# Row tiles on TensorE: scores as two 64x128 tiles, transposes of gathered rows in halves

## The chip, the cores and the metric

The kernel runs on one core of one Trainium2 chip. The metric is the device time of one execution in microseconds; lower is better. TensorE multiplies a stationary operand (loaded first, by a weight load) with a moving operand that is streamed through it. Its 128x128 array can be used as several smaller tiles: a tile is written rows x columns, where the rows are the partitions that are summed over and the columns are the width of the stationary operand.

## The reference

One layer of graph attention over a sparse graph of 2048 nodes, for a batch of 8 and 4 heads of 64 channels, and a second attention layer with one head, then residual and layer norms. Cut to what matters here:

```python
h = jnp.einsum('bnc,hdc->bhnd', x, Wh)                  # 8 x 4 x 2048 x 64
scores = jnp.einsum('...nd,...md->...nm', h, h)
attn = softmax(where(mask, scores, -1e16), axis=-1)     # mask: adjacency and the diagonal
out_h = jnp.einsum('...nm,...md->...nd', attn, h) + bh
z = leaky_relu(heads side by side); h2 = z @ Wo.T
# the same attention once more on h2, then layer norm, residual, layer norm
```

Everything is float32. The adjacency is dense only for nodes of low number; the first 56 nodes are the "hub".

## The kernel before

The kernel never forms the projected features for the scores. With G_h = Wh_h^T Wh_h, the score of nodes n and m in head h is x_n^T G_h x_m, so the raw rows of x are the keys, and `columns` (L802 to L806) makes the queries G_h x of a node's own column. The 8 batches are held as 4 (`Q`) pairs of two (`p`), 64 channels each, so that 128 partitions hold both batches of a pair.

It runs in three parts. First (up to about 144 us in the profile) the adjacency is read and turned into lists of up to 128 neighbours for 166 sets of 12 nodes, while `hub_scores` (L585) and `hub_values` (L601) work off the hub's attention over all 16 blocks of 128 nodes. Then comes the loop at L1017 over 83 pairs of sets (`g`), the first layer. Then a third loop (L1351) does the second layer in the same manner.

The loop at L1017 is written out by hand as a software pipeline, under a manual schedule: the order of the calls is the order of each engine's queue. For pair `g`, spread over several turns:
- `gather` (L790) fetches, by an indirect DMA on GpSimd's queue, the rows of the neighbours of each of the two sets (`j`) into `rows[1, s]`, 128 rows by 4 pairs of batches.
- `turn` (L509) transposes a gathered tile with four TensorE transposes of 128x128 into a PSUM tile `tp` of two banks, one bank for each set. It is called twice in a turn, at L1078 and L1083, with `turn_values` (L863) of an older pair between. ScalarE copies `tp` into `xTg` (L1030) in the next turn.
- `scores` (L814) multiplies `xTg` (stationary) with the queries `y` (moving, 48 columns: 12 nodes x 4 heads). The 64 channels of batch `p` are partitions `half(p)`, and the output goes to bank `p`. Each product of 128 neighbours is made as two products of 64 (`r`), which go to the lower and the upper 64 partitions of the output. VectorE adds the mask (`weigh`, L826), ScalarE takes the exponential (`lift`, L833).
- `values` (L846) multiplies the weights with the gathered rows in 128x64 tiles, `invert` divides, `turn_values` (L863) transposes, `project` (L531) applies the heads' weights in 64x64 tiles, `second_maps` (L880) the second layer's weights in 128x64 tiles, `second_rows` (L890) transposes them for the second layer's table.

TensorE's order within a turn is L821 (scores of pair i+1), L531, L846, L880, L890, L806, L512 (four transposes), L863, L512 (four more). PSUM has one buffer for each of the tags T (transposes), S (scores), O and C in this loop.

`hub_scores` has the same form of product: stationary `xT` in 64 channels x 64 nodes, moving `yh` with 224 columns.

Of the kernel before, what the change touches and what calls it, by code (L numbers as in the profile page):

```python
# [30 lines left out]
F32 = mybir.dt.float32  # L31
# [328 lines left out]
def fast_kernel(ctx: ExitStack, tc: tile.TileContext, x, adj, Wh, bh, Wo, bo, gamma, beta, out, flag):  # L360


    nc = tc.nc
    B, N, C = x.shape
    H, D, _ = Wh.shape
    P = 128
    NB = N // P
    Q = B // 2
# [7 lines left out]
    M = SET * H  # L376
# [14 lines left out]
    work = stage.enter_context(tc.tile_pool(name="work", bufs=2))  # L391
# [3 lines left out]
    def two(name, tag="s", **kw):  # L395

        return psum.tile([P, 2, 512], F32, tag=tag, name=name, **kw)

    def half(k):
        return slice(k * 64, (k + 1) * 64)  # L400
# [10 lines left out]
    ident = const.tile([P, P], F32, name="ident")  # L411
# [19 lines left out]
    xT = early.tile([P, Q, N], F32, name="xT")  # L431
# [74 lines left out]
        nc.vector.tensor_copy(woT.rearrange("p q d -> p (q d)"), po[:, 0, :HP * D])  # L506


    def turn(tp, rows):  # L509

        for q in range(Q):
            nc.tensor.transpose(tp[:, q * P:(q + 1) * P], rows[:, q, 1:1 + P], ident)  # L512

    def leaky(cat, n, name):

        z = work.tile([P, HP, 2, n], F32, tag="z", name=name, bufs=3)
        for hp in range(HP):
            nc.scalar.activation(z[:, hp], cat[:, :, hp * n:(hp + 1) * n], AF.Identity, bias=bhp[:, hp:hp + 1], scale=1.0)  # L518
        return z

    def leak(z):
        f = z.rearrange("p q s n -> p (q s n)")
        nc.vector.scalar_tensor_tensor(f, f, SLOPE, f, OP.mult, OP.max)

    def project(ot, cat, n):

        for hp in range(HP):
            for s in range(2):
                for j in range(2):
                    h = 2 * hp + j  # L530
                    nc.tensor.matmul(cat[half(j), s, hp * n:(hp + 1) * n], whT[half(s), h * D:(h + 1) * D],  # L531
                                     ot[half(s), h, :], start=True, stop=True)
# [3 lines left out]
    HW = HUB * H  # L536
# [32 lines left out]
    yh = early.tile([P, 2, 2 * HUB * H], F32, name="yh")  # L569
# [15 lines left out]
    def hub_scores(i, t):  # L585
        sp = two(f"sh{i}_{t}")
        for k in range(2):
            for p in range(2):
                for r in range(2):
                    nc.tensor.matmul(sp[half(r), p, k * HW:(k + 1) * HW],  # L590
                                     xT[half(p), 2 * t + k, i * P + r * 64:i * P + (r + 1) * 64],
                                     yh[half(p), t, k * HW:(k + 1) * HW], start=True, stop=True)
        e = es[t][:, :4 * HW]
        nc.vector.tensor_tensor(e.rearrange("p (a k n) -> p a k n", a=2, k=2),  # L594
                                sp[:, :, :2 * HW].rearrange("p a (k n) -> p a k n", k=2),
                                maskh[:, i, :].unsqueeze(1).unsqueeze(1).to_broadcast([P, 2, 2, HW]), OP.subtract)
        nc.scalar.activation(e, e, AF.Exp, bias=shifts[:, 0:1], scale=1.0)  # L597
# [189 lines left out]
    rows = {}  # L787
    held = {}
# [23 lines left out]
        nc.scalar.copy(held["y", g // 2][:, :n, g % 2 * 2:g % 2 * 2 + 2], cat[:, :, 2 * GM:2 * GM + n].rearrange("p a n -> p n a"))  # L812

    def scores(g, sp):  # L814
        xt = held.pop(("T", 1, g)).rearrange("c j (q n) -> c j q n", q=Q)
        y = held["y", g // 2][:, g % 2 * GM:(g % 2 + 1) * GM, :].rearrange("p n h -> p (n h)")
        for j in range(2):
            for q in range(Q):
                for p in range(2):
                    for r in range(2):  # L820
                        nc.tensor.matmul(sp[half(r), p, (q * 2 + j) * M:(q * 2 + j + 1) * M], xt[half(p), j, q, half(r)],  # L821
                                         y[half(p), (j * Q + q) * M:(j * Q + q + 1) * M], start=True, stop=True)

    def weigh(g, sp):
        e = es[g % 2]
        nc.vector.tensor_tensor(e[:, :16 * M].rearrange("p (a q n) -> p a q n", a=2, q=Q),  # L826
                                sp[:, :, :8 * M].rearrange("p a (q n) -> p a q n", q=Q),
                                mask[:, 2 * g:2 * g + 2, :].rearrange("p s n -> p (s n)").unsqueeze(1).unsqueeze(1)
                                .to_broadcast([P, 2, Q, 2 * M]), OP.subtract)

    def lift(g):
        e = es[g % 2]
        nc.scalar.activation(e[:, :16 * M], e[:, :16 * M], AF.Exp, bias=shifts[:, 0:1], scale=1.0)  # L833
# [3 lines left out]
    def values(g, op):  # L837
        e = es[g % 2]
        rw = [rows.pop((1, 2 * g + j)) for j in range(2)]
        for q in range(Q):  # L840
            for j in range(2):
                for p in range(2):
                    c0 = (p * 8 + q * 2 + j) * M
                    o0 = q // 2 * OQ + q % 2 * (D + 2) + p

                    nc.tensor.matmul(op[half(p), j, o0:o0 + K1], e[:, c0:c0 + 64], rw[j][:, q, sums(p)], start=True, stop=True)  # L846

    def invert(g, op):
        v = op.rearrange("a j (k c) -> a (j k) c", k=2)[:, :, :2 * (D + 2)].rearrange("a w (s c) -> a w s c", s=2)
        osb = held["o", g] = work.tile([P, 4, 2, D], F32, tag="osb", name=f"osb{g}")  # L850
        r = rall[:, g, :].rearrange("a (w s) -> a w s", w=4)
        for p in range(2):
            nc.vector.reciprocal(r[half(p)], v[half(p), :, :, p * K1])  # L853
        nc.vector.tensor_tensor(osb, v[:, :, :, 1:K1], r.unsqueeze(3).to_broadcast([P, 4, 2, D]), OP.mult)  # L854
# [152 lines left out]
    def one(name, tag):  # L1007
        return psum1.tile([P, 2, 512], F32, tag=tag, name=name)
# [8 lines left out]
    for i in range(-4, NG + 3):  # L1017
        if 0 <= i + 1 < NG:
            sp = one(f"s{i + 1}", "S")
            scores(i + 1, sp)  # L1020
            weigh(i + 1, sp)
        if i >= 1 and slow and len(slow) % 3:
            slow.pop(0)()
        cat = one(f"cat{i}", "C")
        if 0 <= i - 1 < NG:
            project(held.pop(("ot", i - 1)), cat, GM)
            held["z", i - 1] = leaky(cat, GM, f"z{i - 1}")
        if 0 <= i + 2 < NG:
            t = held["T", 1, i + 2] = work.tile([P, 2, 512], F32, tag="xTg", name=f"xTg{i + 2}", bufs=3)
            nc.scalar.copy(t, held.pop(("tp", i + 2)))  # L1030
        if 0 <= i + 1 < NG:
            lift(i + 1)
        if 0 <= i < NG:
            op = one(f"o{i}", "O")
            values(i, op)
            invert(i, op)
        if 0 <= i + LOOK < NG and i > -3:
            for j in range(2):
                gather(table1, 2 * (i + LOOK) + j, 1, rows_tile)
        if i + 6 < NG and i % 2 == 0 and i >= -2:  # L1040
            own_rows((i + 6) // 2)
        if 0 <= (i - 30) // 2 <= NV:
            (add_beta if i % 2 else load_own)((i - 30) // 2)
        if 0 <= i - 1 < NG:
            leak(held["z", i - 1])
        if i >= 0:
            if turns():
                some(1)
            if slow and len(slow) % 3 == 0:
                slow.pop(0)()  # L1050
            more(1)
            if todo3 and i == todo3[0][0]:
                make_keys(2, todo3.pop(0)[1], late_two)
            if not picks:
                ready = done
            if not picks and not todo3 and done < NS:
                picks = pick(2)
                done = NS
            assert i + 1 + LOOK >= NG or 2 * (i + 1 + LOOK) + 1 < ready

        if 0 <= i - 2 < NG:
            second_maps(i - 2, cat[:, 0, 384:384 + GM])
        if 0 <= i - 3 < NG:
            second_rows(i - 3, cat[:GM, 1, 384:512])
        if 0 <= i + 4 < NG + NG % 2:
            columns(i + 4, cat)
        if 0 <= i - 2 < NG:
            keep_own(i - 2, cat[:, 0, 384:384 + GM])
        if 0 <= i - 3 < NG:
            keep_rows(i - 3, cat[:GM, 1, 384:512])  # L1070
        for _ in range((2 if i < 22 or i % 2 else 1) if i >= 0 else 0):
            if not turns():
                some(1)
        if 0 <= i + 4 < NG + NG % 2:
            keep_columns(i + 4, cat)
        if 0 <= i + 3 < NG:
            tp = held["tp", i + 3] = one(f"t{i + 3}", "T")
            turn(tp[:, 0, :], rows[1, 2 * (i + 3)])  # L1078
        if 0 <= i < NG:
            turn_values(i, op)  # L1080
            keep_values(i, op)
        if 0 <= i + 3 < NG:
            turn(tp[:, 1, :], rows[1, 2 * (i + 3) + 1])  # L1083
    assert not picks and not pieces and not todo3 and done == NS
    begin.close()
    stage.close()
# [347 lines left out]
```

## Time and profile before

| | us |
|---|---|
| median of 3 runs | 879.14 (877.95 to 882.98) |
| the profiled execution, its own time | 880.76 |
| its span from first to last instruction | 878.9 |
| PE busy in the span | 753.0 |
| PE busy between 190 and 582 us | 385.8 of 392 |
| mean granted clock of TensorE | 0.951 |

PE stands for TensorE's matmuls and transposes, PEld for its weight loads, DVE for VectorE, ACT for ScalarE, POOL for GpSimd. A row such as "PE s L821 x64" in the chain of waits means 64 instructions of line 821 that write the tile `s`. In rows of instructions "64*64 64x48" is the shape of the stationary operand and of the moving one. Matmuls overlap: a single one's duration is longer than the time between two starts, so the length of a group on the chain, or the distance between starts, tells what it costs.

### The profile page before, as it was taken

Reading aid. Unit: us, or ns where it says so; the run is one execution under the profiler, and the core shown is the slowest. Engines: PE = TensorE matmul, PEld = TensorE weight load, DVE = VectorE, ACT = ScalarE, POOL = GpSimd, SP = SyncE. Lnnn points to the kernel's source line nnn. Section 1 sums busy time; section 2 is a strip of 40 time slices with the busy share of each in tenths; the row PEclk is TensorE's granted clock in tenths of the full one; section 3 lists DMA queues with packets and bytes.
Section 4 is the critical chain, followed back from the end, with each engine's and each line's share of the span. In section 5 each row is a group of like instructions: output and inputs, shape, how many; then the busy total and the mean of one; then the engine's idle time right before and its main releaser. Section 6 shows DMA issues by size and latency. Waiting matters only on the chain.

```text
span 878.9 us, 42066 instructions
## 1 busy us (share of the span) xinstructions
PE 753.0 (86%) x18437; PEld 661.2 (75%) x18437; DVE 610.1 (69%) x1369; ACT 514.4 (59%) x961; POOL 469.2 (53%) x612
## 2 busy tenths in 40 slices
PE   1896777889999999999999999992999999998730
PEld 1664456778788999988999999971899999988720
DVE  3356983568888788877555555553258999998994
ACT  2342333556556667666766667651678888886821
POOL 5654141457444555655666666503777777777300
PEclk9998998999999999999999999995999999999965
DMA  8787451355434445655566665514888888888611
GB/s 167 238 218 213 129 146 48 83 142 160 109 100 118 112 125 159 162 169 153 160 168 173 160 166 162 134 28 114 246 266 253 275 275 267 266 252 242 172 46 35
DMA packets 81794, 145.22 MB, mean 165 GB/s; under 512 B 30146, under 2 KB 46466, under 8 KB 81602
## 3 DMA queue, kind: packets, MB, share of 16 engines
q0 software_dynamic: 26720, 88.55, 36.4%
q1 hardware_dynamic: 37842, 49.65, 18.7%
q10 hardware_dynamic: 17040, 4.25, 2.6%
q8 instruction: 147, 2.41, 1.1%
q14 instruction: 45, 0.37, 0.1%
HBM read 123.91 MB, written 18.48 MB: 162 GB/s over the span
## 4 chain that ended last, share of the span: by engine, by line
PE 63%; DVE 15%; DMA 7%; ACT 5%; issue 4%; SPq 3%; POOL 2%; DVEq 0%; ACTq 0%; POOLq 0%
PE t L512 11%; PE s L821 10%; PE o L846 10%; PE cat L806 6%; PE o L863 4%; PE cat L531 4%; PE cat L880 3%; PE s L1133 3%; PE o L1165 3%; PE cat L890 2%; DMA raw<-in_adj_dram 2%; SPq L1248 2%; PE sh L1277 2%; PE e L1144 2%; DMA g<-table,index 1%
## 5 line engine op out<-in xcount | busy, mean ns | idle before, releaser
L792 POOL DMA_INDIRECT g<-table,index x332 | 334.9, 1009 | 236.1 <-PE o L846 140.2
L512 PE MATMUL t<-ident,g 128*128 128x128 f32 x1328 | 182.3, 276 | 15.6 <-DMA g<-table,index 12.7
L512 PEld LDWEIGHTS t<-ident,g 128*128 128x128 f32 x1328 | 154.8, 142 | 20.0 <-issue 14.0
L826 DVE TENSOR_TENSOR e<-s,mask 128x768 f32<-128x768 f32 x83 | 79.4, 956 | 87.4 <-PE s L821 85.4
L518 ACT ACTIVATE z<-cat,bhp 128x192 f32<-128x192 f32 x166 | 60.8, 418 | 85.0 <-PE cat L531 85.0
L846 PE MATMUL o<-g,e 128*64 128x65 f32 x2656 | 97.5, 227 | 0.0
L821 PEld LDWEIGHTS s<-y,xTg 64*64 64x64 f32 x5312 | 85.2, 134 | 13.9 <-issue 13.7
L821 PE MATMUL s<-y,xTg 64*64 64x48 f32 x5312 | 95.5, 220 | 0.0
L846 PEld LDWEIGHTS o<-g,e 128*64 128x64 f32 x2656 | 85.8, 140 | 9.8
L1320 ACT COPY xTg<-t 128x1024 f32<-128x1024 f32 x83 | 80.3, 1017 | 18.1 <-PE t L512 17.3
L1030 ACT COPY xTg<-t 128x1024 f32<-128x1024 f32 x83 | 84.0, 1012 | 2.0 <-PE t L512 2.0
L833 ACT ACTIVATE e<-e,shifts 128x768 f32<-128x768 f32 x83 | 79.2, 955 | 2.1 <-DVE e L826 1.7
L812 ACT COPY y<-cat 128x384 f32<-128x384 f32 (+1 forms) x80 | 40.7, 508 | 64.0 <-PE o L863 40.1
L597 ACT ACTIVATE e<-e,shifts 128x896 f32<-128x896 f32 x32 | 33.4, 1042 | 73.0 <-DVE e L594 52.1
L680 POOL TENSOR_SCALAR a<-raw 120x1024 bf16<-120x1024 int32 (+1 forms) x34 | 38.2, 1125 | 65.1 <-DMA raw<-in_adj_dram 38.4
L806 PE MATMUL cat<-xo,gram 128*128 128x192 f32 (+1 forms) x320 | 65.6, 328 | 0.0
L853 DVE RECIPROCAL rall<-o 64x8 f32<-64x8 f32 x166 | 34.0, 205 | 42.0 <-PE o L846 40.7
L854 DVE TENSOR_TENSOR osb<-o,rall 128x512 f32<-128x512 f32 x83 | 57.4, 692 | 2.9
L1165 PE MATMUL o<-g,es 128*32 128x65 f32 x2656 | 49.1, 226 | 5.9 <-DVE y_s L1188 4.5
L806 PEld LDWEIGHTS cat<-xo,gram 128*128 128x128 f32 x320 | 53.7, 203 | 0.3 <-issue 0.2
L1165 PEld LDWEIGHTS o<-g,es 128*32 128x32 f32 x2656 | 46.1, 113 | 7.0 <-issue 4.9
L1133 PE MATMUL s<-xTg,bd 128*32 128x128 f32 x1328 | 45.4, 277 | 6.2 <-ACT bd L1124 3.5
(177 smaller groups left out, 1369.3 us busy)
## 6 DMA issues: line engine op xcount, KB each, us to landing
raw<-in_adj_dram SPq DMA_DIRECT2D x32, 480.0 KB
table<-xb SPq DMA_DIRECT2D x22, 256.0 KB
xr_s<-table SPq DMA_DIRECT2D x21, 256.0 KB
g<-table,index POOLq DMA_INDIRECT x332
table<-x SPq DMA_DIRECT2D x16, 260.0 KB
x<-in_x_dram ACTq DMA_DIRECT2D x32, 128.0 KB
table<-rowt SPq DMA_DIRECT2D x166, 24.4 KB
xb<-in_x_dram SPq DMA_DIRECT2D x164, 24.0 KB
```

The costliest lines, as they stand in the source:

```text
L512: nc.tensor.transpose(tp[:, q * P:(q + 1) * P], rows[:, q, 1:1 + P], ident)
L518: nc.scalar.activation(z[:, hp], cat[:, :, hp * n:(hp + 1) * n], AF.Identity, bias=bhp[:, hp:hp + 1], scale=1.0)
L792: nc.gpsimd.indirect_dma_start(out=t.rearrange("n q c -> n (q c)"), out_offset=None, in_=table, in_offset=bass.IndirectOffsetOnAxis(ap=ind ...
L806: nc.tensor.matmul(cat[:, k, 2 * GM:2 * GM + n], gram[:, g % 2 * 2 + k, :], held["x", g // 2][:, :n], start=True, stop=True)
L821: nc.tensor.matmul(sp[half(r), p, (q * 2 + j) * M:(q * 2 + j + 1) * M], xt[half(p), j, q, half(r)], y[half(p), (j * Q + q) * M:(j * Q + q ...
L826: nc.vector.tensor_tensor(e[:, :16 * M].rearrange("p (a q n) -> p a q n", a=2, q=Q), sp[:, :, :8 * M].rearrange("p a (q n) -> p a q n", q= ...
L833: nc.scalar.activation(e[:, :16 * M], e[:, :16 * M], AF.Exp, bias=shifts[:, 0:1], scale=1.0)
L846: nc.tensor.matmul(op[half(p), j, o0:o0 + K1], e[:, c0:c0 + 64], rw[j][:, q, sums(p)], start=True, stop=True)
L1030: nc.scalar.copy(t, held.pop(("tp", i + 2)))
L1133: nc.tensor.matmul(sp[q * 32:(q + 1) * 32, k, :], bd[u % 3][:, k, q, :], xt[:, s % 2, q, :], start=True, stop=True, tile_position=(0, q * 32))
L1165: nc.tensor.matmul(op[t * 32:(t + 1) * 32, f, k * W2 + p:k * W2 + p + K1], e[:, 2 * q + p, k, :], rw[:, q, sums(p)], start=(a == 0 and k = ...
L1320: nc.scalar.copy(t, tp)
```

## The change

Three products change shape; what is computed stays.

`scores` and `hub_scores` drop the loop over `r`: one product has 128 neighbours as its stationary operand and writes all 128 partitions of bank `p`. Its tile is 64 rows by 128 columns instead of 64 by 64, and there are half as many.

The transposes of gathered rows in the loop at L1017 go through a new function. Each transposes 64 of the 128 gathered rows, so its tile is 64x128 as well, and the two halves (`r`) of a tile write to different banks of `tp`. The copy at L1030 puts the halves side by side again; it moves the same 1024 elements in each partition. The second layer's transposes and those of x stay whole.

```diff
+    def turn_halves(tp, rows, j):
+
+        for q in range(Q):
+            c0 = (j * Q + q) * 64
+            for r in range(2):
+                nc.tensor.transpose(tp[:, r, c0:c0 + 64], rows[half(r), q, 1:1 + P], ident[half(r), half(r)])
...
     # hub_scores
-                for r in range(2):
-                    nc.tensor.matmul(sp[half(r), p, k * HW:(k + 1) * HW],
-                                     xT[half(p), 2 * t + k, i * P + r * 64:i * P + (r + 1) * 64],
-                                     yh[half(p), t, k * HW:(k + 1) * HW], start=True, stop=True)
+                nc.tensor.matmul(sp[:, p, k * HW:(k + 1) * HW], xT[half(p), 2 * t + k, i * P:(i + 1) * P],
+                                 yh[half(p), t, k * HW:(k + 1) * HW], start=True, stop=True)
...
     # scores
-        xt = held.pop(("T", 1, g)).rearrange("c j (q n) -> c j q n", q=Q)
+        xt = held.pop(("T", 1, g)).rearrange("c (j q) n -> c j q n", q=Q)
...
-                    for r in range(2):
-                        nc.tensor.matmul(sp[half(r), p, (q * 2 + j) * M:(q * 2 + j + 1) * M], xt[half(p), j, q, half(r)],
-                                         y[half(p), (j * Q + q) * M:(j * Q + q + 1) * M], start=True, stop=True)
+                    nc.tensor.matmul(sp[:, p, (q * 2 + j) * M:(q * 2 + j + 1) * M], xt[half(p), j, q, :],
+                                     y[half(p), (j * Q + q) * M:(j * Q + q + 1) * M], start=True, stop=True)
...
-            t = held["T", 1, i + 2] = work.tile([P, 2, 512], F32, tag="xTg", name=f"xTg{i + 2}", bufs=3)
-            nc.scalar.copy(t, held.pop(("tp", i + 2)))
+            t = held["T", 1, i + 2] = work.tile([P, 2, 512], F32, tag="xTg", name=f"xTg{i + 2}", bufs=3).rearrange("c j (q n) -> c (j q) n", n=P)
+            nc.scalar.copy(t.rearrange("c m (r n) -> c r m n", r=2), held.pop(("tp", i + 2)).rearrange("c r (m n) -> c r m n", n=64))
...
-            turn(tp[:, 0, :], rows[1, 2 * (i + 3)])
+            turn_halves(tp, rows[1, 2 * (i + 3)], 0)
...
-            turn(tp[:, 1, :], rows[1, 2 * (i + 3) + 1])
+            turn_halves(tp, rows[1, 2 * (i + 3) + 1], 1)
```

## Prediction, made before the changed kernel ran

> **What bounds the kernel now.** I read the page first, then the busy time by stretches, then the chain of waits inside the long middle stretch, then the weight loads one by one. The page gives one engine that is nearly full, and says where:
>
> ```profile
> PE 753.0 (86%) x18437; PEld 661.2 (75%) x18437; DVE 610.1 (69%) x1369; ACT 514.4 (59%) x961; POOL 469.2 (53%) x612
> PE   1896777889999999999999999992999999998730
> ...
> PEclk9998998999999999999999999995999999999965
> ...
> PE t L512 11%; PE s L821 10%; PE o L846 10%; PE cat L806 6%; PE o L863 4%; PE cat L531 4%; PE cat L880 3%; PE s L1133 3%; PE o L1165 3%; PE cat L890 2%; DMA raw<-in_adj_dram 2%; SPq L1248 2%; PE sh L1277 2%; PE e L1144 2%; DMA g<-table,index 1%
> ```
>
> ```profile
> 190.00:582.00 392.00, 385.78 (x10397) 349.55 (x10399) 278.78 (x718) 256.57 (x529) 222.21 (x294) 1.00 0.54 145
> ```
>
> The first number group of the second fence is the stretch, then busy us of PE, PEld, DVE, ACT, POOL, the granted clock (1.00) and DMA. From 190 to 582 us PE is busy 385.8 of 392 us and no other engine exceeds 279. This is the loop over the 83 pairs of sets. All three edited places feed it, except the hub's scores before it. The chain of waits there holds nothing but PE; one turn of the loop reads:
>
> ```profile
> 465.43 1.08 PE s L821 x64
> 466.51 0.35 PE cat L531 x16
> 466.85 1.08 PE o L846 x32
> 467.94 0.33 PE cat L880 x8
> 468.27 0.25 PE cat L890
> 468.51 0.65 PE cat L806 x4
> 469.17 0.44 PE t L512 x4
> 469.60 0.38 PE o L863 x4
> 469.99 0.44 PE t L512 x4
> ```
>
> That is 5.00 us a turn, all of it TensorE. The scores are on the chain for 10% of 878.9 us, 88 us, which at 1.08 us is 81 of the 83 turns. So whatever TensorE gains or loses in a turn counts about 81 times, and changes on other engines count for nothing: the copy at L1030 keeps its 1024 elements (1.01 us), and ScalarE is busy 257 of 392 us.
>
> **What a step of TensorE costs.** A float32 matmul appears as two instructions (64 for 32 calls at L821); a transpose as one. From the start times of single instructions in the same trace:
> - A stream of N columns costs 0.85 ns a column: a full transpose of 128 columns starts every 109 ns, 192 columns (L806) every 163 ns.
> - Four 64x64 tiles start within 20 ns of each other and then the same four start again 58 ns later. Their 48 columns would need 41 ns, so the columns do not set this; the next load into the same tile does.
> - L806 shows the same limit for 128-column weights, in the one group that has only 96 columns to stream: its loads start 112 ns apart, where the stream needs 82. L1277 (120-column weights, 112 streamed) steps in 105 ns.
>
> ```profile
> 574.01 0.42 PE cat L806 x4
> ```
>
> Four instructions in 0.42 us is 105 ns each, against 0.65 us for four of 192 columns. So the load costs 58 ns for 64 columns, 105 for 120, 112 for 128.
> - Transposes load faster. Where PE had been waiting, two loads of 128-column transposes start 56 to 65 ns apart, 76 times in the trace; and L863 streams its 112 columns in 95 ns steps with 128-column weights, which a 112 ns load would forbid.
>
> **What a change of tile shape costs.** The weight-load row idles only where the tile shape changes:
>
> ```profile
> 464.83 0.36 PEld L512 LDWEIGHTS t<-ident,g 128*128 128x128 f32 x3
> 465.36 1.02 PEld L821 LDWEIGHTS s<-y,xTg 64*64 64x64 f32 x64 [0.17 <-issue]
> 466.29 0.38 PEld L531 LDWEIGHTS cat<-otb,whT 64*64 64x64 f32 x16
> ```
>
> Between L821 and L531 (both 64*64) the steps run through. At the three changes of a turn the next group starts late, and its second step is late too, since the first load is exposed: L512 to L821 93 + 36 = 129 ns, L531 to L846 110 + 50 = 160, L880 to L890 101 + 41 = 142 over the undisturbed step. Mean 143 ns.
>
> **The change, part by part, in one turn.**
> Scores: 64 instructions of 64x64 in 16 rounds of four become 32 of 64x128 in 16 rounds of two. The number of rounds stays; a round is now one 128-column load in each row tile. 16 x (112 - 58) = +0.85 us. Below, the bound is 0 (the load in a half-height tile as quick as now); above, the two row tiles load one after the other, 32 x 112 - 16 x 58 = +2.65 us. I take +0.85: tiles of both row halves load within 20 ns of each other today, so two row tiles should overlap, and the nearest row for a 128-column float32 load is L806's 112 ns.
>
> Transposes: 8 of 109 ns become 16 halves in 8 rounds of two, each half streaming 64 columns (54 ns) behind a 128-column load. With the quick load a round takes 58 ns: 8 x 58 - 8 x 109 = -0.41 us. With a 112 ns load it is +0.02. I take -0.41, from the rows of the transposes themselves, which differ only in height. The Trainium skill's page "TensorE: Matmul & The Clock Gate", section "LDWEIGHTS (loading the stationary operand)", gives a load as its columns over 1.2 GHz, whatever the number of rows. That fits the 58, 105 and 112 ns here and speaks against this change; for transposes the measured 56 to 65 ns contradict it. By the page, estimated, a half would cost 107 ns and this term would be near nothing, the whole then about 985 us.
>
> Changes of shape: the order in a turn stays L806, transposes, L863, transposes, scores, L531, L846, L880, L890. The transposes are now 64x128 between two full-size groups. New changes: L806 to transposes, transposes to L863, L863 to transposes, scores to L531 (64x128 to 64x64). Gone: transposes to scores. 4 x 143 - 129 = +0.44 us. Bounds: +0.01 if passing between 64x128 and 128x128 is free (then one old change is only replaced by another), +0.51 at 160 ns each. No row shows this pair of shapes; all three changes that the trace has cost alike, so I take +0.44. The page "TensorEngine Tiling (Array Packing)", section "Key Properties", says that changing the tiling mode drains the engine; it lists 64x128 as a configuration of its own, which would speak for the higher bound, and no run shows it yet.
>
> Hub's scores: 224 columns take 190 ns a round, more than the 112 ns load, so the number and length of rounds stay; the exposed first load grows by 112 - 58 = 54 ns in each of 32 groups. That is 1.7 us at most, and the chain before 144 us is mostly DMA, VectorE and GpSimd with 4% for L590, so I count 0.
>
> Sum: 0.85 - 0.41 + 0.44 = +0.88 us a turn, x 81 = +71 us. Against the profiled execution's 880.8 us that is 952; the median of the runs is 879.1, 1.7 lower, hence 950.
>
> No wait moves: the change adds none, the copy at L1030 still waits for the last transpose of a turn, and a longer turn only gives VectorE, ScalarE and the gathers on GpSimd more slack.
>
> **The rivals.**
> - Half-height transposes load at the ordinary rate (112 ns). Against it the 76 short pairs; for it, that every one of them has full height. +0.85 + 0.02 + 0.44 = 1.31 x 81 = +106, 985 us.
> - Passing between 64x128 and 128x128 is free, as both use whole columns. 0.85 - 0.41 + 0.01 = 0.45 x 81 = +37, 916 us. Against it: nothing but the three changes that do cost.
> - The other side: a 128-column float32 load into a half-height tile takes no longer than today's four 64-column ones, 58 ns, which already bring 128 columns into each row half, and shape changes between full-column tiles are free. Then only the transposes' gain is left: -0.39 x 81 = -32, 847 us. It decides as soon as the score round is below some 63 ns (16 rounds x 5 ns are 0.08 us) with the drains gone. L806 and L1277 speak against it. With quick loads but drains as today the sum is -0.41 + 0.44, +3 us: 882, no change.
> - Row tiles don't overlap their loads: +2.65, 16 x 58 - 8 x 109 = +0.06, +0.44: 3.15 x 81 = +255, 1134 us.
>
> **How the numbers follow.** Forecast 0.62; slow half transposes 0.13; free passing 0.12; faster 0.06; quick loads with drains 0.03; serial loads 0.04. The forecast's own range is 925 to 975 (drains at 110 to 160 ns, 78 to 83 turns). Stretched to the two neighbours, 908 to 990, it leaves out about 0.15. The measurement tells some 0.5%, 4.4 us, from no change: faster 0.06, same 0.03, slower 0.91.
>
> **What would show it.** Right: a turn of 5.9 us on a chain still all PE; the scores' piece near 1.9 us with half the instructions; each group of eight half transposes near 0.23 us plus a late start; weight-load idle before the transposes, L863 and L531. Wrong: the scores still at 1.1 us (loads quick), no idle before L863 (passing free), half transposes at 0.45 us a group (slow loads), scores over 3 us (no overlap), or a turn that ends on another engine.

## The result, and the profile after

| | us |
|---|---|
| before, median of 4 runs | 878.84 |
| after, median of 4 runs | 956.09 (952.12 to 959.59) |
| ratio | 1.087, 95% interval 1.082 to 1.092 |
| profiled execution after: its own time, its span | 958.55, 956.7 |

The change costs 77 us. The forecast was 950, with 908 to 990 as its range. The page of the changed kernel, the lines that answer to those shown of before (line numbers moved; L825 are the scores, L514 the half transposes, L867 the transposes of the quotients, formerly L863):

```profile
PE 832.6 (87%) x16189; PEld 721.6 (75%) x16189; DVE 611.8 (64%) x1369; ACT 514.8 (54%) x961; POOL 464.1 (49%) x612
...
PE s L825 16%; PE o L850 9%; PE t L514 7%; PE cat L811 6%; PE o L867 5%; PE cat L538 4%; PE t L519 4%; PE s L1137 3%; PE cat L884 3%; PE o L1169 3%; PE cat L894 2%; PE e L1148 2%; PE sh L1281 2%; ACT xTg L1324 1%; SPq L1252 1%
...
L825 PE MATMUL s<-y,xTg 64*128 64x48 f32 x2656 | 164.1, 274 | 0.0
L825 PEld LDWEIGHTS s<-y,xTg 64*128 64x128 f32 x2656 | 158.6, 192 | 0.1
...
L514 PE MATMUL t<-ident,g 64*128 64x64 f32 x1328 | 77.2, 238 | 2.4 <-issue 2.4
```

PE is busy for 80 us more with 2248 fewer instructions; the other engines have the same work. The scores are half as many (2656 for 5312) and now 16% of the chain instead of 10%. One turn of the loop on the chain of waits of the changed kernel:

```profile
505.86 1.77 PE s L825 x32
507.63 0.49 PE cat L538 x16
508.13 1.08 PE o L850 x32
509.21 0.33 PE cat L884 x8
509.54 0.24 PE cat L894
509.78 0.65 PE cat L811 x4
510.44 0.39 PE t L514 x8
510.83 0.53 PE o L867 x4
511.36 0.40 PE t L514 x8
```

This turn is 5.90 us, all TensorE, against 5.00; the medians over the loop are 5.89 and 5.00. Scores +0.69, transposes 0.39 + 0.40 instead of 0.88, the quotients 0.53 for 0.38 and the heads' products 0.49 for 0.35: these last two do the same work, and only start late. The weight loads show where the late start is. Before:

```profile
463.52 0.35 PEld L806 LDWEIGHTS cat<-xo,gram 128*128 128x128 f32 x2
463.84 0.52 PEld L512 LDWEIGHTS t<-ident,g 128*128 128x128 f32 x4
```

After:

```profile
509.95 0.19 PEld L811 LDWEIGHTS cat<-xo,gram 128*128 128x128 f32 x1
510.37 0.33 PEld L514 LDWEIGHTS t<-ident,g 64*128 64x128 f32 x8 [0.23 <-issue]
510.76 0.39 PEld L867 LDWEIGHTS o<-ident,osb 112*128 112x128 f32 x4
511.29 0.33 PEld L514 LDWEIGHTS t<-ident,g 64*128 64x128 f32 x8
511.53 1.87 PEld L825 LDWEIGHTS s<-y,xTg 64*128 64x128 f32 x32
```

Before, the loads of the transposes followed those of L806 (now L811) without a gap. Now 0.23 us pass before them. Between the second group of transposes and the scores, both 64*128, there is none.

The loop, from the first masking operation on VectorE to the last, went from 432.7 us (153.3 to 586.0) to 505.7 (154.1 to 659.8): +73.0. From the first to the last there are 82 steps, and at +0.89 each they make 73. Another 4 us came after the loop.

### The profile page after: what moved, and what is told of

Same layout as the page of the kernel before. It is cut to its first block, busy times and chain, and to the rows that moved or that the text cites. A ratio compares the mean times of both kernels' runs of the same rounds, so it can differ in the third digit from the quotient of the medians.

```text
span 956.7 us, 37570 instructions
## 1 busy us (share of the span) xinstructions
PE 832.6 (87%) x16189; PEld 721.6 (75%) x16189; DVE 611.8 (64%) x1369; ACT 514.8 (54%) x961; POOL 464.1 (49%) x612
## 4 chain that ended last, share of the span: by engine, by line
PE 70%; DVE 12%; DMA 4%; ACT 4%; issue 4%; POOL 2%; SPq 2%; ACTq 1%; DVEq 0%; POOLq 0%
PE s L825 16%; PE o L850 9%; PE t L514 7%; PE cat L811 6%; PE o L867 5%; PE cat L538 4%; PE t L519 4%; PE s L1137 3%; PE cat L884 3%; PE o L1169 3%; PE cat L894 2%; PE e L1148 2%; PE sh L1281 2%; ACT xTg L1324 1%; SPq L1252 1%
## 5 line engine op out<-in xcount | busy, mean ns | idle before, releaser
L825 PE MATMUL s<-y,xTg 64*128 64x48 f32 x2656 | 164.1, 274 | 0.0
L825 PEld LDWEIGHTS s<-y,xTg 64*128 64x128 f32 x2656 | 158.6, 192 | 0.1
L525 ACT ACTIVATE z<-cat,bhp 128x192 f32<-128x192 f32 x166 | 60.8, 418 | 154.1 <-PE cat L538 154.1
L519 PE MATMUL t<-ident,g 128*128 128x128 f32 x664 | 84.3, 280 | 12.9 <-DMA g<-table,index 11.8
L519 PEld LDWEIGHTS t<-ident,g 128*128 128x128 f32 x664 | 76.7, 145 | 15.1 <-issue 12.3
L514 PEld LDWEIGHTS t<-ident,g 64*128 64x128 f32 x1328 | 54.8, 140 | 33.1 <-issue 20.9
L514 PE MATMUL t<-ident,g 64*128 64x64 f32 x1328 | 77.2, 238 | 2.4 <-issue 2.4
L811 PE MATMUL cat<-xo,gram 128*128 128x192 f32 (+1 forms) x320 | 65.7, 328 | 0.0
L811 PEld LDWEIGHTS cat<-xo,gram 128*128 128x128 f32 x320 | 53.7, 202 | 0.2 <-issue 0.2
```

The costliest lines, as they stand in the source:

```text
L514: nc.tensor.transpose(tp[:, r, c0:c0 + 64], rows[half(r), q, 1:1 + P], ident[half(r), half(r)])
L811: nc.tensor.matmul(cat[:, k, 2 * GM:2 * GM + n], gram[:, g % 2 * 2 + k, :], held["x", g // 2][:, :n], start=True, stop=True)
L825: nc.tensor.matmul(sp[:, p, (q * 2 + j) * M:(q * 2 + j + 1) * M], xt[half(p), j, q, :], y[half(p), (j * Q + q) * M:(j * Q + q + 1) * M], s ...
```

## The experiments

Two theories of the loss stand against each other. The forecast's: a round of scores costs its weight load, and every change of tile shape drains the array. Its rivals: fewer tiles in flight leave the array idle whatever their width; the late starts are waits for data or banks; the halves themselves are slow.

**One part at a time.** The loop's scores alone:

```diff
-                        nc.tensor.matmul(sp[half(r), p, ...], xt[half(p), j, q, half(r)], y[half(p), ...])
+                    nc.tensor.matmul(sp[:, p, ...], xt[half(p), j, q, :], y[half(p), ...])
```

> Only the loop's scores go to two 64x128 tiles; transposes stay whole, the hub's scores stay 64x64. Theory (a round costs its weight load, and every change of tile shape some 145 ns): 16 rounds x (112 - 58) = +0.86 us; the change from transposes to scores stays one, the step from scores to the heads' products becomes a new change, +0.14. Together +1.0 us a turn, x 81 = +81 us: about 960 us, that is slower than or level with the whole change. Rival (the transposes in halves are what costs, the scores are neutral): within 10 us of before.

Measured: 960.1 us, ratio 1.090 (1.084 to 1.095). The turn is 5.98 us, +0.98. By the turn the scores alone cost slightly more than the whole change (5.89); the times of the two (956.7 to 961.6 and 952.1 to 959.6 us) overlap.

The transposes alone (`turn_halves` with its copy, scores and hub's scores as before):

> Only the transposes of gathered rows go to halves; both scores stay 64x64. Theory: rounds of 58 to 60 ns give -0.40 us a turn; three more changes of tile shape at about 145 ns give +0.43: +0.03 us a turn, +2 us, 881 us, no change that can be told. Rival 1 (row halves are simply twice as fast, the late starts are waits that would be there anyway): -0.40 x 81 = -32, 847 us. Rival 2 (halves don't share the array well): slower than 890.

Measured: 885.5 us, ratio 1.0057 (1.0026 to 1.0088). A turn:

```profile
504.57 1.08 PE s L828 x64
505.65 0.35 PE cat L538 x16
505.99 1.08 PE o L853 x32
507.07 0.33 PE cat L887 x8
507.41 0.24 PE cat L897
507.65 0.65 PE cat L813 x4
508.30 0.39 PE t L514 x6
508.70 0.53 PE o L870 x4
509.23 0.39 PE t L514 x8
```

5.05 us, +0.05 (x6 in place of x8: the trace lacks two records): the halves' gain and three new late starts cancel, and the kernel is a little slower. Neither rival of this run came.

The hub's scores alone:

> Only the hub's scores go to two 64x128 tiles. Theory: a round streams 224 columns in 190 ns, longer than a 112 ns load, so rounds stay, and only the exposed first load grows, 32 x 54 ns = 1.7 us at most, mostly beside DMA and VectorE: 879 to 881 us. Rival (what the whole change lost beyond 81 turns x 0.90 us, some 5 us, sits in the hub's part): 883 to 885 us.

Measured: 881.4 us, ratio 1.001 (0.998 to 1.004). No change that can be told, so the 4 us beyond the loop are not shown to be there; the interval ends at 3.5 us.

**What sets a round of scores.** The same number of products in the same tile and banks, only narrower (one line of the edit; the mask and the exponential also work on 96 partitions, and the other 32 get a constant weight):

```diff
-                    nc.tensor.matmul(sp[:, p, ...], xt[half(p), j, q, :], ...)
+                    nc.tensor.matmul(sp[:96, p, ...], xt[half(p), j, q, :96], ...)
```

> The whole change, with scores for the first 96 of the 128 listed neighbours only (the stationary operand has 96 columns, the mask and the exponential work on 96 partitions, the other 32 neighbours get a constant weight); the number of products, their tile, the 48 streamed columns and the banks stay. Theory (the width of the load sets the round): a round goes from 112 to 85 ns (96 columns at the 0.83 ns a column that 64 against 128 columns show, and 5 ns); 16 x -27 = -0.43 us a turn, x 81 = -35 us: about 921 us. Rival (two tiles in flight instead of four leave the array idle, whatever the width): rounds stay at 112, 953 to 960 us.

The whole time (7243 us) can't be used: the profile shows the general kernel running behind the fast one (L205, L229, L245), which the program does when sums leave its limits. The loop itself ran as meant:

```profile
505.78 0.39 PE t L514 x8
506.17 0.53 PE o L867 x4
506.70 0.39 PE t L514 x8
507.09 1.35 PE s L825 x32
508.44 0.49 PE cat L538 x16
```

Scores 1.35 for 1.77 us, a median turn of 5.46 for 5.89: -0.43, as the load's width said. Rounds start 85 ns apart. The theory of fewer tiles in flight forecast no change. So the width of the stationary operand sets the round: 58, 85 and 112 ns for 64, 96 and 128 columns, at 48 streamed columns throughout.

**Do row tiles overlap because of their order?**

```diff
-        for q in range(Q):
-            for r in range(2):
+        for r in range(2):
+            for q in range(Q):
```

> The whole change, with the half transposes of a tile ordered lower half of all four pairs first, then the upper halves, so that neighbours in the queue share a row tile. Theory (a half costs its 58 ns load in its own row tile and only different row tiles overlap): if the queue is taken in order, each group of eight needs 8 x 58 instead of 4 x 60 ns, +0.23 us, twice a turn, +0.45 x 81 = +37 us: about 993 us. Rival (the gain is that only 64 columns are streamed, not the overlap; or the queue looks far enough ahead): 953 to 960 us.

Measured: 959.1 us (two runs), turn 5.90, each group 0.40 us. My expectation was wrong and the rival right. The first two loads of a group start 13 ns apart. The rows do not name the row tile, but two loads of whole transposes, which share one tile, started 56 ns or more apart; so I read the second load as the other row tile's, although four transposes of the first tile stand ahead of it. The order of neighbours is no lever here.

**What the late starts are.** First, the quotients (L867) ahead of both groups of halves, so that two changes of shape go:

```diff
+            turn_values(i, op)
+            keep_values(i, op)
             turn_halves(tp, rows[1, 2 * (i + 3)], 0)
-            turn_values(i, op)
-            keep_values(i, op)
             turn_halves(tp, rows[1, 2 * (i + 3) + 1], 1)
```

> The whole change, with the transposes of L863 (turn_values) put ahead of both groups of half transposes instead of between them; no product changes. Theory (changes of tile shape cost): L806 to L863 becomes no change, L863 to the halves stays one, the halves run on into each other and into the scores; two changes of some 145 ns are gone, -0.29 us a turn, x 81 = -23 us: about 933 us, a turn of 5.6 us. Rival (the late starts of L863 and of the second group are waits for VectorE's quotient and for the gathers, or bank conflicts, and not the shape): 950 to 960, or slower, as L863 now asks for the quotient 0.4 us earlier.

Measured: 945.9 us, ratio 1.076 (1.073 to 1.080): -10 us against the whole change instead of -23, a turn of 5.84. Both theories had a share. The two groups of halves run through (0.64 us for sixteen, against 0.39 and 0.40), but L867 starts 349 ns after the last L811, where 163 ns is the undisturbed step, and its second step is 56 ns late: 0.24 us lost for some 0.29 gained. These turns explain 4 of the 10 us. Most of the rest lies at the loop's start: its first five turns took 33.5 us instead of 39.7, with a granted clock of 0.91 instead of 0.50 from 150 to 155 us. The same order with 64x64 scores:

> Scores and hub's scores as before the change (64x64), the gathered rows transposed in halves, and L863 put ahead of both groups. Theory: halves -0.40 us a turn; L806 to L863 no change, L863 to the halves one new change of 145 ns, the halves to the scores one in place of the old one: -0.26 us a turn, x 81 = -21 us: about 858 us. Rival (the order makes L863 wait for the quotient): the gain is eaten, 875 to 885 us.

Measured: 896.5 us, ratio 1.022 (1.017 to 1.027), far off the 858 expected. What the quotients' transposes (there L870) wait for stands in the timeline:

```profile
500.88 0.69 DVE L861 TENSOR_TENSOR osb<-o,rall 128x512 f32<-128x512 f32 x1
501.62 0.40 PEld L870 LDWEIGHTS o<-ident,osb 112*128 112x128 f32 x4 [0.32 <-DVE osb L861]
```

The quotient ends at 501.57 and TensorE starts at once. Moved ahead, the transposes meet data that is not ready: the median turn is 5.01 us, as long as before the change. The 17 us above that lie in pauses in which PE waits for nothing that the profile shows, 22.9 us between 200 and 640 us against 2.6 before; the largest row of its table of waits (us in total, times, longest) is

```profile
PE o L853 <- issue: 16.4, 17, 1.8
```

This order can't tell what a change of shape costs. So I gave the quotients the rows' tile shape instead, and left the order, and with it the waits (the main lines of the edit; the copy `otb` behind them comes in four pieces instead of two):

```diff
-            nc.tensor.transpose(turned(op)[:, w, :], osb[:112, w]..., ident[:112, :112])
+            for p in range(2):
+                rws = slice(p * 64, p * 64 + M)
+                nc.tensor.transpose(op[:, p, c0:c0 + M], osb[rws, w]..., ident[rws, rws])
```

> The whole change, with the quotients of L863 also transposed in half-height tiles and the order kept. Theory: against the whole change two changes of shape less, -0.29, and quotients -0.15: -0.44 us a turn, x 81 = -36 us: about 920 us, a turn of 5.46 us; no late start before L863 or after it. Rival (the late starts are waits): 945 to 957.

Measured: 920.2 us, ratio 1.045 (1.038 to 1.051), with a median turn of 5.47, as expected. That the time agrees to a microsecond is luck: the first turns ran at a higher clock than in the changed kernel here too (0.81 from 150 to 155 us).

```profile
505.17 0.40 PE t L514 x8
505.56 0.23 PE o L870 x8
505.80 0.26 PE t L514 x8
506.06 1.77 PE s L825 x32
```

Here L870 follows L514 with no late start, and the second group takes 0.26 instead of 0.40 us. It waits for the same quotient as in the changed kernel, at a slightly earlier moment, and the second group writes the same banks as there; so the late starts were the change of tile shape.

**A kernel faster than both?** The same with 64x64 scores:

> Scores 64x64 as before; the gathered rows and also the quotients of L863 (turn_values) are transposed in half-height tiles, in the order of the changed kernel (rows, quotients, rows), so that the three groups share one tile shape and L863 asks for the quotient no earlier. Theory (changes of shape cost, waits don't move): rows -0.40 us a turn; quotients 4 x 58 instead of 4 x 96, -0.15; one new change of shape (L806 to the halves) +0.14: -0.41 us a turn, x 81 = -33 us, about 847 us. Rival 1 (the late starts around L863 are its wait for the quotient): -0.15 at most against the transposes alone, 870 to 880. Rival 2 (instructions can't be fetched faster; the pauses without a visible cause seen with the quotients moved ahead come back): 865 to 890 with 'issue' waits on PE.

Measured: 879.6 us, ratio 0.997 (0.993 to 0.9998): hardly anything of the 33 us. Between 300 and 580 us the turn's median is 4.89 us, its mean 5.10 (before: 5.00 and 5.04). Two things took the gain. One is a second chain: `rall` and `osb` are the reciprocals and the quotients, L530 is the leaky ReLU (`leak`) of `z`, `own` and `rowt` make the rows of the second layer's table, `y` the queries, and `otb` is the copy of the turned quotients that the heads' products (L538) read. In its timeline:

```profile
508.44 0.42 DVE L860 RECIPROCAL rall<-o 64x8 f32<-64x8 f32 x2 [0.69 <-PE o L853]
508.90 0.69 DVE L861 TENSOR_TENSOR osb<-o,rall 128x512 f32<-128x512 f32 x1
509.51 0.55 DVE L530 SCALAR_TENSOR_TENSOR z<-z 128x384 f32<-128x384 f32 x1
509.97 0.25 DVE L896 COPY own<-cat 128x96 f32<-128x96 f32 x1
510.14 0.28 DVE L905 TENSOR_TENSOR rowt<-cat,bob 96x128 f32<-96x128 f32 x1
510.51 0.51 ACT L819 COPY y<-cat 128x384 f32<-128x384 f32 x1 [0.66 <-DVE rowt L905]
510.91 0.67 ACT L881 COPY otb<-o 128x96 f32<-128x96 f32 x4
511.63 0.37 PEld L538 LDWEIGHTS cat<-otb,whT 64*64 64x64 f32 x16 [0.16 <-ACT otb L881]
```

From the end of the values to the end of the copy `otb` it takes 3.18 us (median), then the heads' products start 0.05 us later and the next values follow: 4.88 us around. Of the 3.18, 0.13 come from `otb` in four pieces (0.67 us for 0.54). Before the change the same chain ended 0.25 us ahead of its need (it took 3.05; L531's first load came at 3.35, and 0.05 is the time to start). The other thing is the pauses named in the table of waits as "issue": 7.8 us between 300 and 580 us, 0.2 before. To take the first away, the leak of z (L530) went behind the row copy:

> The kernel with scores 64x64 and rows and quotients in half-height transposes, and on VectorE the leak of z (L530, 0.55 us, of which 0.47 on the chain) moved behind the row copy that the second layer's table waits for. Theory (with the transposes in halves a second chain sets the turn: values, VectorE's reciprocals, quotient, leak, own, row, then ScalarE's copies of y and of the turned quotients, 3.18 us, then the heads' products and the next values): without the leak that chain is some 0.47 us shorter, TensorE sets the turn again at about 4.6 us, -0.4 x 81 = -33 us against before less some 10 us of pauses in which PE waits for nothing that shows: 850 to 865 us. Rival (pauses of instruction supply, not that chain, hold the turn): 875 to 885 us, as without the move.

Measured: 869.8 us, ratio 0.9895 (0.986 to 0.993), faster than both kernels, by 1% against the one before, though short of 850 to 865. An undisturbed turn is 4.67 us, and between 300 and 580 us the median is 4.82 and the mean 5.03. The theory was right in part only. The second chain became shorter by 0.21 us, 2.97 for 3.18, and not by the 0.47 expected:

```profile
515.89 0.26 DVE L896 COPY own<-cat 128x96 f32<-128x96 f32 x1 [0.17 <-PE cat L813]
516.43 0.51 ACT L819 COPY y<-cat 128x384 f32<-128x384 f32 x1 [0.45 <-PE o L873]
516.83 0.67 ACT L881 COPY otb<-o 128x96 f32<-128x96 f32 x4
517.55 0.37 PEld L538 LDWEIGHTS cat<-otb,whT 64*64 64x64 f32 x16
```

`own` now waits for TensorE's L813, and the profile puts the wait of `y` down to its L873. The heads' products still start 0.05 us after the end of `otb`, so in an undisturbed turn this chain still ends last. The longest pauses that are left in PE's table of waits, 300 to 580 us:

```profile
PE o L853 <- issue: 7.1, 9, 1.1
PE cat L891 <- issue: 2.8, 4, 1.2
```

The columns are us in total, times, longest. In the kernel before, the same stretch has "issue" only once, 0.2 us. As a control, the move of the leak in the kernel before:

> The kernel before, with nothing but the leak of z moved behind the row copy on VectorE. Theory (before the change TensorE sets the turn at 5.00 us and the chain over VectorE and ScalarE ends 0.3 us before the heads' products can start): no change, 876 to 883 us. Rival (the move by itself is what made the last kernel faster): 865 to 873 us.

Measured: 882.7 us, ratio 1.003 (0.9998 to 1.006): no gain. TensorE set the turn there, and a shorter second chain is worth nothing until the first has shrunk.

The second layer's rows in halves as well (on top of the kernel of 879.6 us):

> As the kernel with scores 64x64 and rows and quotients in halves, and the second layer's gathered rows in halves too. Theory: a unit of four sets has 16 transposes, 1.75 us; in halves 16 x 58 ns, -0.8, one new change of shape +0.14: -0.66 us for each of 42 units where TensorE sets the pace; VectorE is busy 37 of 40 us there and takes over after some 3 of 40, so -8 to -20 us against the same kernel without it: 827 to 840 us. Rival (the second layer is paced by VectorE or the gathers already): no change against it.

Measured: 886.2 us, ratio 1.005 (1.002 to 1.008), no gain. The second layer became no shorter: from the last masking operation of the first layer to the end it is 299 us for 293. Between 700 and 740 us PE is busy 33.7 instead of 38.2 us, VectorE 34.6 and 36.5:

```profile
700.00:740.00 40.00, 33.71 (x1041) 29.58 (x1029) 34.60 (x61) 31.08 (x54) 29.55 (x30) 1.00 0.87 267
```

The first busy number is PE, the third VectorE. There VectorE and ScalarE take the chain over: between 660 and 820 us they hold 94 us of it instead of 27, TensorE 43 instead of 113.

## Why the prediction was right, step by step

- **The bound.** Right: all nine pieces of a turn are TensorE before and after, 82 steps of +0.89 us explain the loop's 73.0 us. That they do so to a fraction of a us is partly luck: a slow start of the loop and later turns that gave it back cancel (see the last section).
- **Scores, +0.85.** Rounds start 112 ns apart as taken from L806, 16 of them, and two row tiles start 3 ns apart, so they overlap. The run with 96 columns shows that it is the width. The piece on the chain grew by only 0.69, because its own first load is no longer exposed; that is booked under the changes of shape.
- **Transposes, -0.41.** Rounds take 58 to 62 ns. The price was taken from pairs of full-height loads that happened to be free, 56 to 65 ns apart, and held at half height. The Trainium skill's page "TensorE: Matmul & The Clock Gate", section "LDWEIGHTS (loading the stationary operand)", gives a load as its columns over 1.2 GHz whatever the number of rows, an estimated 107 ns for 128 columns. That is near the products' loads here (112 ns) and not the transposes' (58 to 62 ns).
- **Changes of shape, +0.44.** From start to start, the late first and second steps are in the median 95 + 51 ns (L811 to L514), 94 + 56, 94 + 50 and 93 + 51 (L825 to L538): 144 to 150 each, 143 forecast. The scores' own start is undisturbed. The page "TensorEngine Tiling (Array Packing)", section "Key Properties", states that changing the tiling mode drains the engine. The late starts agree with it, 94 and 95 ns between 64x128 and 128x128 as well, which was open.
- **The sum, +0.88.** Measured +0.89. The total missed by 6 us: 2 from the loop (73 for 71), 4 from outside it. The latter are not settled. At the start of the second layer PE's clock was granted at 0.50 from 689 to 694 us in this run, a stretch that had 0.71 in the run before. The prediction's inner range, 925 to 975, is wider than what it names as its source: drains of 110 to 160 ns over 78 to 83 turns give some 938 to 958.
- **No wait moves.** Right for this change. It would have been wrong for any faster version: 0.25 us behind TensorE stood a chain over VectorE and ScalarE that the prediction did not look for, since the change was forecast to lengthen the turn.

## What to carry to other kernels

Count rounds, not instructions: with the 48 streamed columns here a round cost the load of the stationary operand, so joining two 64-column tiles into one of 128 halved the instructions and nearly doubled the time of the round (58 to 112 ns). Lay products of one tile shape next to each other and price each change of shape; here four new ones for one old cost 0.44 us a turn, more than the 0.41 that transposes twice as fast gained. And before a bound engine is made faster, measure how far behind it the next chain ends: here 0.25 us of 5.

## What the hardware showed that I had not expected

- Loads of transposes and loads of float32 products differ: 128 columns in 58 to 62 ns against 112 ns.
- TensorE seems to look ahead in its queue over at least four transposes and their loads to start the other row tile (two loads start 13 ns apart; that the second is the other tile's is inferred).
- Pauses grew where more instructions ran in less time. Between 200 and 575 us, steps of over 0.5 us from one start on TensorE to the next add up to 7.6 us before, 12.6 with the transposes alone, 24.0 in the fastest kernel; in such pauses the profile names no cause for 2.4, 6.3 and 13.4 us. In the fastest kernel 16 of 24 end 2.1 to 2.7 us after the start of the latest 16 KB transfer on the instruction queue (some 3 would by chance, with 86 transfers in 375 us), before the change 1 of 8. That points to instruction supply; it was not tested by itself.
- The granted clock can stay at 0.50 while PE is recorded as busy throughout. At the loop's start in the changed kernel:

```profile
150.00:155.00 5.00, 5.00 (x49) 4.91 (x46) 0.90 (x1) 1.18 (x2) 0.12 (x1) 0.50 0.27 88
155.00:160.00 5.00, 5.00 (x51) 4.47 (x50) 0.06 (x1) 2.35 (x3) 0.00 (x0) 0.50 0.01 3
```

The kernel before was granted 0.97 and 1.00 in these stretches. The first five turns took 39.7 us against 31.4, some 3.8 us more than 0.89 a turn explains; later turns, which had more idle time before the change, gave it back. Why the clock stayed low there is open.
